# A planned four-layer graph network: planner constants and order tables made anew

## The chip, the cores and the metric

The kernel runs on one core of a Trainium2 chip, as one launch. The metric is the device time of that launch in microseconds. Three runs of the kernel before gave 2421.40, 2421.62 and 2425.13 us, median 2421.62.

## What is computed

128 graphs of 128 nodes with 512 features go through four graph layers; after each the input is added back and the rows are layer-normalised. x is (128, 128, 512), adj (128, 128, 128), everything in float32. Cut to what matters:

```python
x = layernorm(x + relu(An @ x @ K + b))          # layer 0, An = D^-1/2 (adj + I) D^-1/2
x = layernorm(x + softmax_n(w) * (x @ Wv.T))     # layer 1, w = sum_m (q k^T / 8 * adj)
x = layernorm(x + relu(cat(x, adj @ x / deg) @ W.T))   # layer 2
x = layernorm(x + An @ (x @ W3 + b3))            # layer 3
```

The outputs are the last x, (128, 128, 512).

## The kernel before

**Tiling.** Four graphs form a group; there are 32 groups, numbered 0 to 31. One group's x is a tile of 128 partitions (nodes) by four graphs of 512 features. The weight products use a scheme of seven block products in place of eight: each weight is kept as seven blocks of 128 x 2 x 256 (`B11`, `T1`, ..., line 31), the sums of blocks of the data (names with `s1`, `s2`, `s4`, `xT1s`, `xT2s`, `agg0s`, `agg3s`, `inners`) are made by VectorE and GpSimd, and seven products, numbered 0 to 6, are accumulated for each tile. So `p_o0:3` is the fourth unit of matmuls of the layer 0 product of a group, `p_v` that of layer 1, `p_2x` and `p_2g` those of layer 2, `p_o3` that of layer 3, and `p_agg0`, `p_agg3` are the products with the adjacency.

**Weights.** Layer 0's and layer 3's weights, with their sums, do not stay on chip: they are stored once to a scratch tensor in DRAM (`w0d`, `w3d`; function `keep`, line 1009) and fetched again in seven pieces of 256 KB for each group into `wz_sb` (`fetch`, line 1013). A third scratch tensor, `w2d`, holds part of layer 2's weight. Layer 2's weight comes in pieces of 32 KB into `wa_sb`, `wb_sb`, `wc_sb` and `w2y` (`load_w2`, line 1024); `w2_sums` (line 1035) adds the blocks.

**Loops.** After a start with the first groups, a loop over t (lines 1760 on) records layers 0 and 1 of group t beside layers 2 and 3 of group t−1, so in the steady part four layers of work of two groups stand side by side: one such period is one group's time.

**Transposes** of x for layers 1 and 2 mostly go by DMA through a scratch tensor in DRAM (store `xT1s`/`xT2s`, load `xT1y`/`xT2y`, then a block transpose on VectorE into `xT`; `turn_x`, line 1169); in the first groups and the last they are done on PE (`p_xT1`, `p_xT2`; `turn_on_tensor`, line 1183). The adjacency with its scale is `ana`, transposed `anT`; `arT` is the plain one transposed; `sa` and `ya` carry it through a scratch tensor for the attention scores. `p_w`, `scr`, `e_sb`, `p_ws` are the softmax of layer 1; `square`, `last1o`, `last3o`, `last4o`, `mvo`, `rstdo` belong to the layer norms.

**What sets the order.** Nothing is issued as the program text is read. Every call is recorded as an operation of a plan (`Plan.record`, line 666). `Plan.schedule` (line 704) then builds due times, moves some operations to another engine, and `Plan.run` (line 783) plays all operations against a cost estimate and writes down the order in which each engine would take them. `Plan.emit` (line 887) issues them in that order; each engine then works through its own list strictly in order, and an operation that waits holds up all that stand behind it. Since all are issued from `emit`, nearly every row of the profile has line 890, and names of tiles tell the operations apart. Five things steer the plan:

- `estimate` (line 914) gives each operation its duration; for a DMA an issue time on SyncE, 400 ns here, and a size from the length of its runs (`PACKET`).
- `HEAD, BUS` (line 641): in the plan a DMA's data moves at the rate `BUS[0]` if it is issued in the first 40000 ns, at `BUS[1]` after that. `FLIGHT` limits the DMAs under way, `LAND` is added to each.
- `EARLY` (line 33) has a number for each operation of a group, in units of 100 ns, by which its due time is put forward or back. Keys are engine, name and count, such as `s:sa:0c`. A last letter tells the group: `w` for operations of no group (weights), `a`, `b`, `c` for groups 0, 1, 2, none for 3 to 29, `y` for 30, `z` for 31. The first letter is the engine the operation was recorded for (`g` GpSimd, `v` VectorE, `s` ScalarE or SyncE, `t` PE).
- `MOVED` (line 419) lists operations that `move` (line 766) hands to another engine: a sum between VectorE and GpSimd, a copy or a normalisation from ScalarE to VectorE.
- `TIMES` (line 457) fixes, for groups 3 to 29, the order of each engine: an offset for each operation, repeated every `PERIOD` of 73637 ns for the next group.

Group suffixes are used below where an operation of one of the first groups is meant: `p_2g` of group 0, `p_agg3_0` of group 0 and so on.

Of the kernel before, what the change touches and what calls it, by code (L numbers as in the profile page):

```python
# [33 lines left out]
    "g:agg0:0": 52, "g:agg0:0b": 110, "g:agg0:0c": -35, "g:agg0:0y": -5, "g:agg0:0z": -425, "g:agg0s1:0": 31,  # L34
    "g:agg0s1:0b": 134, "g:agg0s1:0c": 107, "g:agg0s1:0y": 132, "g:agg0s1:0z": 84, "g:agg0s2:0": 12,
    "g:agg0s2:0b": -210, "g:agg0s2:0c": 123, "g:agg0s2:0y": -361, "g:agg0s2:0z": -261, "g:agg0s4:0": -71,
    "g:agg0s4:0b": -79, "g:agg0s4:0c": 87, "g:agg0s4:0y": 360, "g:agg0s4:0z": 859, "g:agg30:0z": 623,
    "g:agg30s1:0z": 410, "g:agg30s2:0z": 646, "g:agg30s4:0z": 77, "g:agg31:0z": -329, "g:agg31s1:0z": 410,
    "g:agg31s2:0z": 392, "g:agg31s4:0z": 766, "g:agg3:0": 131, "g:agg3:0a": 333, "g:agg3:0b": -88, "g:agg3:0c": -110,
    "g:agg3:0y": -322, "g:agg3s1:0": 75, "g:agg3s1:0a": 528, "g:agg3s1:0b": -174, "g:agg3s1:0c": -73,  # L40
    "g:agg3s1:0y": -982, "g:agg3s2:0": 6, "g:agg3s2:0a": 24, "g:agg3s2:0b": 233, "g:agg3s2:0c": -16,
    "g:agg3s2:0y": 633, "g:agg3s4:0": 130, "g:agg3s4:0a": -4, "g:agg3s4:0b": 225, "g:agg3s4:0c": -489,
    "g:agg3s4:0y": -118, "g:arT:0": -6, "g:arT:0a": 45, "g:arT:0b": -500, "g:arT:0c": -40, "g:arT:0y": -264,
    "g:arT:0z": -170, "g:arT:1": 52, "g:arT:1a": -19, "g:arT:1b": -120, "g:arT:1c": -597, "g:arT:1y": -412,
    "g:arT:1z": 241, "g:d:0": 24, "g:d:0a": 202, "g:d:0b": 597, "g:d:0c": -98, "g:d:0y": 479, "g:d:0z": 577,
    "g:inner:0": 28, "g:inner:0a": -23, "g:inner:0b": 33, "g:inner:0c": -161, "g:inner:0y": -103, "g:inner:0z": -9,
    "g:inner:1": 32, "g:inner:1a": 163, "g:inner:1b": 49, "g:inner:1c": -147, "g:inner:1y": -81, "g:inner:1z": 158,
    "g:inner:2": 62, "g:inner:2a": 14, "g:inner:2b": 333, "g:inner:2c": 228, "g:inner:2y": -362, "g:inner:2z": -769,
    "g:inners1:0": -21, "g:inners1:0a": 207, "g:inners1:0b": 311, "g:inners1:0c": -84, "g:inners1:0y": 211,
    "g:inners1:0z": 1020, "g:inners1:1": 69, "g:inners1:1a": -28, "g:inners1:1b": -19, "g:inners1:1c": 429,  # L50
    "g:inners1:1y": -160, "g:inners1:1z": 52, "g:inners2:0": 6, "g:inners2:0a": 42, "g:inners2:0b": 316,
    "g:inners2:0c": -125, "g:inners2:0y": 934, "g:inners2:0z": 495, "g:inners2:1": 27, "g:inners2:1a": 22,
    "g:inners2:1b": 597, "g:inners2:1c": -319, "g:inners2:1y": 431, "g:inners2:1z": 201, "g:inners4:0": 15,
    "g:inners4:0a": 206, "g:inners4:0b": -185, "g:inners4:0c": 151, "g:inners4:0y": -376, "g:inners4:0z": -365,
    "g:inners4:1": 4, "g:inners4:1a": 46, "g:inners4:1b": 343, "g:inners4:1c": 17, "g:inners4:1y": 855,
    "g:inners4:1z": 35, "g:last3o2_0:0": -2, "g:last3o2_0:0a": -168, "g:last3o2_0:0b": -312, "g:last3o2_0:0c": 71,
    "g:last3o2_0:0y": -1126, "g:last3o2_0:0z": -8300, "g:last3o2_0:1": -5, "g:last3o2_0:1a": -191,
    "g:last3o2_0:1b": 131, "g:last3o2_0:1c": -27, "g:last3o2_0:1y": -274, "g:last3o2_0:1z": -11, "g:last3o2_0:2": -4,
    "g:last3o2_0:2a": -32, "g:last3o2_0:2b": 253, "g:last3o2_0:2c": 125, "g:last3o2_0:2y": 103,
    "g:last3o2_0:2z": -362, "g:last3o3_0:0": 15, "g:last3o3_0:0a": -230, "g:last3o3_0:0b": -70,  # L60
    "g:last3o3_0:0c": -256, "g:last3o3_0:0y": -437, "g:last3o3_0:0z": -808, "g:last3o3_0:1": 22,
    "g:last3o3_0:1a": 380, "g:last3o3_0:1b": -258, "g:last3o3_0:1c": -80, "g:last3o3_0:1y": 1086,
    "g:last3o3_0:1z": 703, "g:last3o3_0:2z": -4121, "g:last3o3_0:3z": 2795, "g:last3o3_1:0z": -1845,
    "g:last3o3_1:1z": 1419, "g:last4o2_0:0": 6, "g:last4o2_0:0a": -46, "g:last4o2_0:0b": -18, "g:last4o2_0:0c": 320,
    "g:last4o2_0:0y": 1210, "g:last4o2_0:0z": 8290, "g:mean_w3:0w": 2, "g:mean_wv:0w": 265, "g:rs:0": -117,
    "g:rs:0a": -100, "g:rs:0b": -43, "g:rs:0c": 86, "g:rs:0y": -127, "g:rs:0z": 357, "g:rstdo0_0:0": 25,
    "g:rstdo0_0:0a": -173, "g:rstdo0_0:0b": 183, "g:rstdo0_0:0c": -144, "g:rstdo0_0:0y": -134, "g:rstdo0_0:0z": -584,
    "g:rstdo0_0:1": 10, "g:rstdo0_0:1a": 160, "g:rstdo0_0:1b": 126, "g:rstdo0_0:1c": 291, "g:rstdo0_0:1y": 1688,
    "g:rstdo0_0:1z": 572, "g:rstdo0_1:0": 36, "g:rstdo0_1:0a": -417, "g:rstdo0_1:0b": 180, "g:rstdo0_1:0c": 120,
    "g:rstdo0_1:0y": -1819, "g:rstdo0_1:0z": -632, "g:rstdo0_1:1": 28, "g:rstdo0_1:1a": 463, "g:rstdo0_1:1b": 20,  # L70
    "g:rstdo0_1:1c": -257, "g:rstdo0_1:1y": 3996, "g:rstdo0_1:1z": 1836, "g:rstdo3_1:0z": -238, "g:rstdo3_1:1z": 2729,
    "g:v1_0:0": 175, "g:v1_0:0a": -3, "g:v1_0:0b": -122, "g:v1_0:0c": 161, "g:v1_0:0y": 536, "g:v1_0:0z": 159,
    "g:v1_0:1": 53, "g:v1_0:1a": -235, "g:v1_0:1b": -130, "g:v1_0:1c": -458, "g:v1_0:1y": -20, "g:v1_0:1z": -54,
    "g:v1_1:0": 2, "g:v1_1:0a": -127, "g:v1_1:0b": -359, "g:v1_1:0c": 283, "g:v1_1:0y": 352, "g:v1_1:0z": 545,
    "g:v1_1:1": -20, "g:v1_1:1a": 3, "g:v1_1:1b": -110, "g:v1_1:1c": 140, "g:v1_1:1y": 268, "g:v1_1:1z": 73,
    "g:v2_0:0": -25, "g:v2_0:0a": -357, "g:v2_0:0b": -330, "g:v2_0:0c": 69, "g:v2_0:0y": -202, "g:v2_0:0z": 138,
    "g:v2_1:0": -30, "g:v2_1:0a": 50, "g:v2_1:0b": 165, "g:v2_1:0c": -151, "g:v2_1:0y": 1510, "g:v2_1:0z": 553,
    "g:w2y1:0w": -79, "g:wa_sb:0w": -55, "g:wb_sb:0w": 48, "g:wb_sb:1w": -280, "g:wb_sb:2w": -90, "g:wb_sb:3w": -170,
    "g:wc_sb:0w": 73, "g:wc_sb:1w": 11, "g:wc_sb:2w": 88, "g:wc_sb:3w": -88, "g:wc_sb:4w": -224, "g:wc_sb:5w": -90,
    "g:xT1:0": -66, "g:xT1:0a": 56, "g:xT1:0b": 74, "g:xT1:0c": -108, "g:xT1:0y": -179, "g:xT1:0z": 469,  # L80
    "g:xT1s1:0": 17, "g:xT1s1:0a": 259, "g:xT1s1:0b": 113, "g:xT1s1:0c": 400, "g:xT1s1:0y": 2729, "g:xT1s1:0z": 1624,
    "g:xT1s2:0": -8, "g:xT1s2:0a": 40, "g:xT1s2:0b": -109, "g:xT1s2:0c": -136, "g:xT1s2:0y": -182, "g:xT1s2:0z": 378,
    "g:xT1s4:0": 19, "g:xT1s4:0a": 169, "g:xT1s4:0b": 19, "g:xT1s4:0c": 3, "g:xT1s4:0y": 257, "g:xT1s4:0z": 172,
    "g:xT2:0": 25, "g:xT2:0a": -1190, "g:xT2:0b": 137, "g:xT2:0c": 150, "g:xT2:0y": -641, "g:xT2:0z": -64,
    "g:xT2:1": 16, "g:xT2:1a": -52, "g:xT2:1b": 897, "g:xT2:1c": 58, "g:xT2:1y": 446, "g:xT2:1z": 651, "g:xT2:2": -34,
    "g:xT2:2a": 54, "g:xT2:2b": -83, "g:xT2:2c": -165, "g:xT2:2y": -342, "g:xT2:2z": 141, "g:xT2s1:0": -35,
    "g:xT2s1:0a": 70, "g:xT2s1:0b": 46, "g:xT2s1:0c": 37, "g:xT2s1:0y": 387, "g:xT2s1:0z": 406, "g:xT2s1:1": 33,
    "g:xT2s1:1a": 218, "g:xT2s1:1b": -344, "g:xT2s1:1c": -47, "g:xT2s1:1y": -1221, "g:xT2s1:1z": -832,
    "g:xT2s2:0": -40, "g:xT2s2:0a": -588, "g:xT2s2:0b": 149, "g:xT2s2:0c": 18, "g:xT2s2:0y": -308, "g:xT2s2:0z": -283,
    "g:xT2s2:1": 47, "g:xT2s2:1a": -167, "g:xT2s2:1b": -30, "g:xT2s2:1c": 52, "g:xT2s2:1y": 1667, "g:xT2s2:1z": 876,  # L90
    "g:xT2s4:0": -25, "g:xT2s4:0a": 166, "g:xT2s4:0b": 536, "g:xT2s4:0c": 103, "g:xT2s4:0y": -764, "g:xT2s4:0z": -38,
    "g:xT2s4:1": 7, "g:xT2s4:1a": -394, "g:xT2s4:1b": -490, "g:xT2s4:1c": 106, "g:xT2s4:1y": -226, "g:xT2s4:1z": 354,
    "s:agg0:0": -59, "s:agg0:0a": -100, "s:agg0:0b": -22, "s:agg0:0c": 4, "s:agg0:0y": 53, "s:agg0:0z": -429,
    "s:agg0:1": 5, "s:agg0:1a": 213, "s:agg0:1b": -168, "s:agg0:1c": -216, "s:agg0:1y": 347, "s:agg0:1z": -324,
# [535 lines left out]
class Plan:  # L630
# [7 lines left out]
    HOP = {"tensor": 150, "vector": 40, "scalar": 40, "gpsimd": 95, "sync": 35}  # L638
    CLOSE = 500
    LAND, FLIGHT = 1700, 9  # L640
    HEAD, BUS = 40000, (0.65, 1)
    PACKET = {32: 16, 128: 33, 256: 82, 512: 102}

    def __init__(self, tc, est):
# [1180 lines left out]
```

## Time and profile before

| quantity | value |
|---|---|
| median of three runs | 2421.62 us |
| profiled execution, its own time | 2425.63 us |
| its span (first to last instruction) | 2423.8 us |
| busy: PE, PE weight load, VectorE | 2358.1, 1938.4, 1759.7 us |
| busy: ScalarE, GpSimd | 1103.7, 1269.4 us |
| granted clock of PE, mean over the span | 0.995 |
| DMA, share of 16 engines, mean rate | 60.7%, 172 GB/s |
| matmuls, DMAs issued on SyncE | 11244, 1809 |

The profiled execution took 4.0 us more than the median of the runs. Its span leaves 1.8 us around it. PE is PE's matmuls, PEld its weight loads, which overlap them; DVE is VectorE, ACT ScalarE, POOL GpSimd, SP SyncE, whose queue issues all the DMAs. Matmul ends are modelled, so PE's busy time is not the time at its peak; the distances between matmul starts are taken instead where a peak rate is wanted. In a row of the timeline, the figure in brackets is how long the engine stood idle before the operation, and what released it.

### The profile page before, as it was taken

Reading aid. Unit: us, or ns where it says so; the run is one execution under the profiler, and the core shown is the slowest. Engines: PE = TensorE matmul, PEld = TensorE weight load, DVE = VectorE, ACT = ScalarE, POOL = GpSimd, SP = SyncE. Lnnn points to the kernel's source line nnn. Section 1 sums busy time; section 2 is a strip of 40 time slices with the busy share of each in tenths; the row PEclk is TensorE's granted clock in tenths of the full one; section 3 lists DMA queues with packets and bytes.
Section 4 is the critical chain, followed back from the end, with each engine's and each line's share of the span. In section 5 each row is a group of like instructions: output and inputs, shape, how many; then the busy total and the mean of one; then the engine's idle time right before and its main releaser. Section 6 shows DMA issues by size and latency. Waiting matters only on the chain. (4 is left out here: it accounts for less than half of the span.)

```text
span 2423.8 us, 35397 instructions
## 1 busy us (share of the span) xinstructions
PE 2358.1 (97%) x11244; PEld 1938.4 (80%) x11244; DVE 1759.7 (73%) x3611; ACT 1103.7 (46%) x2480; POOL 1269.4 (52%) x1571
## 2 busy tenths in 40 slices
PE   8989999999999999999999999999999999999997
PEld 6767778888878878788878888888888888888776
DVE  5876777677777767777776777777776777777776
ACT  4444444444444445444444444444444444444444
POOL 4345465445565455565455555455654455654434
PEclk9999999999999999999999999999999999999998
DMA  5455575666666665666666756665756675756532
GB/s 148 160 154 162 139 210 167 182 171 183 174 200 166 181 182 170 190 187 172 178 180 174 196 166 182 173 195 168 200 169 180 171 190 169 202 163 189 155 113 79
DMA packets 492106, 417.36 MB, mean 172 GB/s; under 512 B 151824, under 2 KB 375312, under 8 KB 491664
## 3 DMA queue, kind: packets, MB, share of 16 engines
q1 hardware_dynamic: 491920, 415.09, 60.7%
q8 instruction: 91, 1.49, 0.3%
q14 instruction: 95, 0.78, 0.1%
HBM read 297.27 MB, written 117.70 MB: 171 GB/s over the span
## 5 line engine op out<-in xcount | busy, mean ns | idle before, releaser
L890 PE MATMUL p_o<-wz_sb,agg 128*128 128x256 f32 x2048 | 477.5, 380 | 10.0 <-DMA wz_sb<-w0d 3.9
L890 PEld LDWEIGHTS p_o<-wz_sb,agg 128*128 128x128 f32 x2048 | 383.7, 190 | 70.3 <-DMA wz_sb<-w0d 10.9
L890 PE MATMUL p_v<-wv_sb,xT 128*128 128x320 f32 x1024 | 297.1, 433 | 1.3 <-DVE xT L890 1.1
L890 PEld LDWEIGHTS p_agg<-anT,x 128*128 128x128 f32 x2048 | 251.7, 196 | 22.9 <-DVE x L890 8.8
L890 PE MATMUL p_agg<-anT,x 128*128 128x128 f32 x2048 | 257.7, 281 | 9.6 <-DVE x L890 7.0
L890 PEld LDWEIGHTS p_v<-wv_sb,xT 128*128 128x128 f32 x1024 | 191.6, 190 | 87.5 <-DVE xT L890 8.7
L890 ACT COPY agg<-p_agg 128x512 f32<-128x512 f32 (+1 forms) x221 | 116.2, 527 | 252.4 <-PE p_agg L890 251.8
L890 PE MATMUL p_v<-wv_sb,xT1s 128*128 128x320 f32 x768 | 228.1, 433 | 1.5 <-POOL xT1s L890 1.1
L890 PEld LDWEIGHTS p_v<-wv_sb,xT1s 128*128 128x128 f32 x768 | 145.2, 190 | 69.9 <-issue 15.1
L890 PE MATMUL p_o<-wz_sb,agg0s 128*128 128x256 f32 x768 | 183.9, 383 | 11.1 <-DMA wz_sb<-w0d 7.6
L890 DVE TENSOR_TENSOR y<-p_2x,y 128x512 f32<-128x512 f32 (+1 forms) x256 | 158.9, 621 | 38.7 <-PE p_2x L890 34.2
L890 POOL TENSOR_TENSOR y<-u,y 128x1024 f32<-128x1024 f32 (+1 forms) x89 | 178.9, 2010 | 15.0 <-DVE u L890 6.0
L890 PE MATMUL p_o<-wz_sb,agg3s 128*128 128x256 f32 x744 | 176.1, 380 | 1.3 <-POOL agg3s L890 1.3
L890 ACT COPY f_2x<-p_2x 128x512 f32<-128x512 f32 (+1 forms) x122 | 64.7, 531 | 246.4 <-PE p_2x L890 239.8
L890 PEld LDWEIGHTS p_o<-wz_sb,agg0s 128*128 128x128 f32 x768 | 142.6, 190 | 42.8 <-issue 16.9
L890 ACT COPY p_2x<-p_2x 128x512 f32<-128x512 f32 (+1 forms) x216 | 109.1, 516 | 115.5 <-PE p_2x L890 67.6
L890 PEld LDWEIGHTS p_o<-wz_sb,agg3s 128*128 128x128 f32 x744 | 138.9, 190 | 20.2 <-POOL agg3s L890 2.5
L890 POOL TENSOR_TENSOR agg3s<-agg 128x512 f32<-128x512 f32 x29 | 36.7, 1267 | 204.6 <-ACT agg L890 202.2
L890 DVE TENSOR_TENSOR v<-p_v,f_v 128x320 f32<-128x320 f32 x128 | 57.5, 485 | 115.0 <-PE p_v L890 114.8
L890 POOL TENSOR_TENSOR agg<-agg 128x512 f32<-128x512 f32 (+1 forms) x32 | 39.7, 1240 | 190.1 <-DVE x L890 158.6
L890 PE MATMUL p_2g<-y,arT 128*128 128x512 f32 x256 | 121.6, 595 | 2.9 <-DVE y L890 1.8
L890 ACT COPY p_o<-p_o 128x512 f32<-128x512 f32 (+1 forms) x96 | 54.1, 564 | 148.2 <-PE p_o L890 144.4
(233 smaller groups left out, 5322.7 us busy)
## 6 DMA issues: line engine op xcount, KB each, us to landing
wz_sb<-w2d SPq DMA_DIRECT2D x224, 256.0 KB, 3.5
wz_sb<-w3d SPq DMA_DIRECT2D x224, 256.0 KB, 3.8
wz_sb<-w0d SPq DMA_DIRECT2D x203, 256.0 KB, 4.1
x<-in_x_dram SPq DMA_DIRECT2D x31, 1024.0 KB, 5.8
out_dram<-x SPq DMA_DIRECT2D x31, 1024.0 KB, 5.1
xT1s<-x SPq DMA_DIRECT2D x120, 256.0 KB, 2.8
xT1y<-xT1s SPq DMA_DIRECT2D x240, 128.0 KB, 2.7
xT2s<-x SPq DMA_DIRECT2D x120, 256.0 KB, 2.7
```

Of the source, the lines that this page charges most:

```text
L890: op.ins = getattr(getattr(self.nc, op.engine), method)(*[v.real() if isinstance(v, Ref) else v for v in args], **{k: v.real() if isinstan ...
```

## The change

Three things differ. The plan's assumed DMA rate for the first 40 us goes from 0.65 to 1.1. A DMA with runs of 256 elements and a size over 1000 in the planner's measure is given 600 ns to issue, no longer 400. And the tables `EARLY`, `MOVED` and `TIMES` hold new numbers throughout: not only the keys of the weights and of groups 0, 1 and 2, but also those of the middle groups and of groups 30 and 31. `PERIOD` stays 73637. The program that records the operations is the same; the number of operations, all the matmuls and all the DMAs are unchanged. Only their order on each engine differs, and for some the engine.

```diff
@@ tables @@
 EARLY = {
-    "g:agg0:0": 52, "g:agg0:0b": 110, "g:agg0:0c": -35, "g:agg0:0y": -5, "g:agg0:0z": -425, "g:agg0s1:0": 31,
...
 TIMES = {
...
     "te": {
-        "p_agg0_3:0": -15388, "p_agg0_1:0": -14793, "p_agg0_0:0": -14186, "p_agg0_2:0": -13424, "p_o0:1": 3745,
-        "p_o0:0": 4975, "p_o0:2": 5558, "p_o0:3": 7384, "p_o0:4": 9773, "p_o0:5": 10599, "p_o0:6": 14335,
...
+        "p_agg0_3:0": -15888, "p_agg0_1:0": -15493, "p_agg0_0:0": -14586, "p_agg0_2:0": -13824, "p_o0:1": 5345,
+        "p_o0:0": 5875, "p_o0:2": 6558, "p_o0:3": 7284, "p_o0:4": 7973, "p_o0:5": 8899, "p_o0:6": 10935,
...
@@ Plan @@
-    HEAD, BUS = 40000, (0.65, 1)
+    HEAD, BUS = 40000, (1.1, 1)
...
@@ estimate @@
     if method == "dma_start":
...
-        return 400, Plan.LAND + size, size, False
+        return 600 if run == 256 and size > 1000 else 400, Plan.LAND + size, size, False
```

As the planned orders come out of it (in each, what stood before and what stands now):

- GpSimd, start: d, ana+ident, ana·d, b0; now ana+ident, d, ana·d, b0. The first ana+ident was tied behind VectorE's dm and is now tied behind dh.
- SyncE, start: ana, b0, wz, x (graphs 2, 3), wz, x (graphs 0, 1) sixth; now ana, x (graphs 0, 1), b0, x (graphs 2, 3), then the four wz pieces.
- SyncE, later: the store `sa` of group 2 stood ahead of most of layer 2's weight pieces, now behind them; the stores of w0d and w3d and the pieces of `wc_sb` come earlier among the others.
- PE, middle groups: 16 of some 72 units stand at another place. Among them, p_o3:3 now stands ahead of p_o0:0, and p_o3:6 ahead of p_o0:3, directly behind p_2x0:0.
- VectorE, middle groups: x of graph 2, row 0 (`x:5`) ahead of `x:7`; `x:19` behind xT2:1, where it stood between xT2:0 and xT2:1.
- Engines, each middle group: three copies of p_o0, f_v_0 and v0 go from VectorE to ScalarE, one normalisation (`x:2`) from ScalarE to VectorE; the sums agg0s4:0, xT1s2:0, arT:0, xT2:1 go from VectorE to GpSimd, inner:0 and xT2:2 from GpSimd to VectorE.

## The prediction

> **What bounds the kernel now.** I read the page first (busy shares), then the table of stretches, then PE's waits, then the timeline where the waits are long. The page and the stretches (columns: stretch, length, then busy us and instructions of PE, weight load, VectorE, ScalarE, GpSimd, then granted clock, DMA share, GB/s):
>
> ```profile
> PE 2358.1 (97%) x11244; PEld 1938.4 (80%) x11244; DVE 1759.7 (73%) x3611; ACT 1103.7 (46%) x2480; POOL 1269.4 (52%) x1571
> ...
> 0.00:20.00 20.00, 13.43 (x76) 12.24 (x76) 5.36 (x12) 4.41 (x9) 7.94 (x15) 0.91 0.84 246
> 20.00:40.00 20.00, 17.20 (x98) 15.17 (x99) 13.80 (x30) 4.93 (x11) 7.93 (x10) 1.00 0.58 171
> ...
> 80.00:100.00 20.00, 20.00 (x105) 16.04 (x103) 16.74 (x28) 8.72 (x20) 7.31 (x7) 1.00 0.31 95
> 100.00:120.00 20.00, 15.87 (x68) 12.38 (x68) 17.14 (x32) 2.24 (x5) 13.45 (x14) 1.00 0.50 162
> 120.00:140.00 20.00, 18.20 (x78) 13.60 (x76) 16.06 (x28) 6.73 (x11) 9.40 (x16) 1.00 0.38 115
> 140.00:160.00 20.00, 11.74 (x54) 10.08 (x53) 12.72 (x38) 11.42 (x29) 4.57 (x8) 0.74 0.81 193
> ```
>
> TensorE bounds it. A 128x256 matmul starts 216 ns after the one before when PE is fed, 128x320 269, 128x512 429, 128x128 111 (starts in the trace); over all matmuls that is 2318.2 of the 2423.8 us span. The matmuls are the same 11244 afterwards, so only the other 105.6 us can move. They lie so: 48.0 before 320 us, about 30 from 320 to 2200, 19.7 after that, and 7 behind the last matmul. PE's waits to 240 us, and from 320 to 2200 us (total, times, longest):
>
> ```profile
> PE p_w L890 <- DVE scr L890: 6.1, 1, 6.1
> PE p_a L890 <- POOL ana L890: 3.4, 1, 3.4
> PE p_o L890 <- DVE u_o L890: 3.4, 3, 1.7
> ...
> PE p_o L890 <- DMA wz_sb<-w0d: 8.7, 27, 1.0
> PE p_2x L890 <- DVE xT L890: 3.7, 8, 1.0
> ```
>
> The head waits for single late things; a middle group (73.6 us) loses only 1.1 to 1.2 us. **The change part by part.** Nothing computed is added or removed: two planner constants change and the tables are new, so order and engine of operations move, in all 32 groups. I walk the new orders with the old durations.
>
> *First 18 us.* GpSimd's old order (timeline: start, length):
>
> ```profile
> 4.67 1.03 POOL L890 TENSOR_TENSOR d<-dh,nhalf 128x4 f32<-128x4 f32 x1 [3.38 <-DVE dh L890]
> ...
> 7.64 1.26 POOL L890 TENSOR_TENSOR ana<-ana,ident 128x512 f32<-128x512 f32 x1 [1.93 <-issue]
> 8.97 1.04 POOL L890 TENSOR_TENSOR ana<-ana,d 128x512 f32<-128x512 f32 x1
> ...
> 10.07 0.66 PE L890 MATMUL p_a<-ident,ana 128*128 128x128 f32 x4 [3.37 <-POOL ana L890]
> ...
> 11.59 5.45 PE L890 MATMUL p_agg<-anT,x 128*128 128x128 f32 x32 [0.86 <-DVE anT L890]
> ```
>
> GpSimd sat still 1.93 us because ana+ident stood behind VectorE's dm (7.50), not for its data. Now ana+ident goes first, behind dh (4.59): 4.67 to 5.93, d to 7.01, ana·d to 8.08, p_a at 8.13 instead of 10.07: **−1.9**. x of graphs 0 and 1 is SP's second issue instead of its sixth; its 512 KB take 5.7 us, so it is there. The wz pieces go back two to four places of 0.6 us and land by about 12.
>
> *Clock.* PE ran at 0.5 from 11.59 to 15.0 here, so the first two graphs' p_agg took 1.87 and 1.63 us, the others 0.89: 1.7 lost. [...] I take half, **−0.9** (ends 0 and −1.9).
>
> *18 to 60.* The four p_agg come earlier and p_o follows in an order whose VectorE copies are ready: by the walk p_agg of group 1 starts near 28.9 (34.7 before), and at 53 us PE is 6 ahead, since 5.4 us of p_v are done earlier in the old gaps (20 to 40 us lost 2.7). SP stood still over 17 us for a store:
>
> ```profile
> 36.21 0.88 SPq L890 DMA_DIRECT2D wa_sb<-in_L_gnn_W_dram  x2
> 54.70 1.31 SPq L890 DMA_DIRECT2D sa<-ana  x2
> ```
>
> The 50-odd 32 KB pieces of layer 2's weights were behind that store; now most go ahead of it at 0.46 us each, and w0d's store near 41 (70.36 before). Price: GpSimd's first wb sum waits for a piece near 55.5, with group 1's rstdo behind it on GpSimd, and PE's transposes of group 1 (p_xT1, 66.5 before) behind that row: **+1.4**. Lead at 60: about 5.
>
> *60 to 140.* w3d's store goes near 63 (77.34), so the sixteen wc pieces that follow land near 80 instead of 93.6. The old sums came in a lump behind them, which is why VectorE is 17.1 of 20 busy exactly where PE is only 15.9:
>
> ```profile
> 93.74 1.23 DVE L890 TENSOR_TENSOR wc_sb<-w2y,wc_sb 128x1024 f32<-128x1024 f32 x1 [0.60 <-DMA wc_sb<-in_L_gnn_W_dram]
> 95.10 2.35 POOL L890 TENSOR_TENSOR wc_sb<-wc_sb,wb_sb 128x1024 f32<-128x1024 f32 x1 [2.68 <-DVE wc_sb L890]
> ...
> 108.43 1.99 PE L890 MATMUL p_o<-wz_sb,agg 128*128 128x256 f32 x8 [1.69 <-DVE u_o L890]
> ```
>
> Spread over 80 to 110 they leave most of the 1.7 + 1.4 + 0.8 us that PE waited for u_o and p_2x between 100 and 120: −3; three new waits for GpSimd's and VectorE's single weight sums, 1.0 + 0.9 + 0.4, give +2.3 back near 112; the wait for w2d's fetch (117 to 122 before) comes earlier with its store: −1.5. Lead at 126: about 9 with all the clock gain, 8 with half.
>
> *140 to 156.* p_w waited 6.1 us, at half clock after it, for scr, which shares a buffer with the squares. The same chain (p_2g, x, four squares, last3o, x) is there in the new order and only starts earlier; ScalarE normalises graph 0's x ahead of graph 1's, which p_agg wants first: −0.7. From 156 to 320 the old order lost about 10 more; I can't walk it to 1 us: 0, ends −3 and +3. **Head: −8.7**, less 1 for the small waits a walk doesn't see: −7.7.
>
> *Middle groups, 27 times.* Each engine swap is one for one within 0.1 us of total: three VectorE copies of 0.48 to 0.68 go to ScalarE (46% busy) and one of 0.80 comes back; three adds go to GpSimd at 1.2 against 0.7 and two come back at 0.7 to 1.3. VectorE, 73% busy, and GpSimd, 52%, hide them; uncovered, one costs its 0.7 us a group. The wait for w0d's fetch at the second p_o tile stays. The one at p_o0:3 (7.1 us in all) goes, as three tiles now stand ahead of it. x of graph 2, row 0, moves ahead on VectorE, so the transposing DMA behind it lands about 0.7 earlier and p_2x0:0's wait (6.6 in all) mostly goes. Against that p_o3:6 now stands right behind p_2x0:0 and needs x:19, which VectorE does behind two xT2 sums, no longer one. Each takes 0.62 from start to start, p_2x0:0 covers 0.4 of it: up to 0.85 us a group; after the 0.55 that the earlier landing spares it is 0.3, 8 in all, or 0.5 and 13 if the DMA lands little earlier. So −5.7, or +6 with that worse end; not seen in the trace, I take a third of the good: **−2**. Tail: −3 to +3, 0 taken.
>
> **Sum**: −7.7 − 2 = −9.7 on the profiled 2425.6, which lies 4.0 above the median of 2421.6: 2415.9 there, **2412** for the median.
>
> **Rivals.** (a) *The lead is lost again* behind the weight sums or the chain at 140, since nothing there is shorter: for it, that chain of 9 us is pure latency; against it, it starts when p_2g ends, earlier. Leaves the 0.7 and 1: 2420. (b) *Only the first 18 us pay*, 1.9 + 0.9, with w2d's fetch as late as before: 2418.5. (c) *Slower: x:19 on VectorE.* If the DMA lands no earlier and PE has no slack there, it waits the whole 0.85 us a group, 23 in all; less the 7.7 of the head and the 7.1 of p_o0:3: +8, 2430. It decides from 0.55 us a group on (14.8 in 27). For it, VectorE is the second busiest and p_o3:6 has no matmul of another tile before it; against it, the sums are due just ahead of the DMA's landing. (d) The constants alone change no program; that nothing moves is out, as the order does.
>
> **Numbers.** Likeliest (head's lead kept, middle within ±6) 0.61, own range 2404 to 2417; (b) 0.11, (a) 0.15, (c) 0.13. 0.2%, 4.8 us, is about what tells from no change. Faster takes the likeliest and half of (b): 0.67; same the rest of (b), (a) and a little of (c): 0.21; slower 0.12. The range leaves out the far side of (c) and gains over 20: 2402 to 2424.
>
> **What would show it.** p_a near 8.1 with GpSimd's 1.93 gone; full clock from 9.6; no SP gap at 37 to 54; w3d near 63; PE over 17 busy in 100 to 120; p_w's 6 us still there, near 132. In the middle, p_o0:3 without w0d and p_o3:6 with a wait for x under 0.4. Wrong if p_2g of group 1 isn't 7 to 10 earlier, or if a middle period is over 73.9.

## The result, and the profile after

The changed kernel takes 2395.14 us (median of four runs, 2393.32 to 2397.90) against 2422.74 for the kernel before on the same chip: a ratio of 0.9886, 95% interval 0.9869 to 0.9903, 27.6 us less. Timed again beside another kernel it had 0.9898 (0.9884 to 0.9912). The forecast was 2412, 9.7 us less, with a range of 2402 to 2424: the sign was right, the size about a third of what came.

The page of the changed kernel:

```profile
PE 2351.7 (98%) x11244; PEld 1941.6 (81%) x11244; DVE 1704.6 (71%) x3506; ACT 1129.1 (47%) x2536; POOL 1306.3 (55%) x1620
```

The matmuls are as many as before; what went is the time between them. To see where, I compare the two traces at equal work: the matmuls done by a given time in the old trace (each counted at its full-rate distance), and how much earlier the new trace has done as many. That is PE's lead, in us:

| old trace's time | 26 | 35 | 60 | 105 | 115 | 126 | 155 | 320 | 1000 | 2200 | 2410 |
|---|---|---|---|---|---|---|---|---|---|---|---|
| lead | 6.3 | 1.6 | 3.2 | 2.2 | 5.2 | 4.5 | 7.1 | 10.1 | 18.0 | 26.7 | 27.1 |

The head gave 10.1, the groups from 320 to 2200 us gave 16.6, the tail 0.4. For the same work, the time between matmuls over full-rate distance fell there from 29.9 to 13.4 us. These are single traces; other kernels with the old tables in the middle lose 28.3 (e11), 27.9 (e10) and 23.9 us (e2) from 320 to 2200, five traces more with the new ones 14.6 to 16.2 (the changed kernel 14.9), so the gain is no chance of two traces, but its size is known to some us only. PE's waits there, after:

```profile
PE p_o L886 <- DMA wz_sb<-w0d: 1.0, 5, 0.3
PE p_o L886 <- DVE x L886: 0.4, 1, 0.4
```

Before, these were 8.7 us for w0d and 3.7 for xT at p_2x. (The list leaves out the shortest waits. In the distances between matmul starts, p_o0:1 went from 9.4 to 6.2 over 25 groups, p_2x0:0 from 5.4 to 0, p_o0:3 from 5.5 to 0, p_o0:2 from 1.8 to 0, and up to 0.1 us a group more went on the matmul behind each.) In the head, the table of stretches after, columns as in the prediction:

```profile
20.00:40.00 20.00, 15.94 (x85) 13.30 (x84) 13.27 (x29) 11.30 (x33) 7.45 (x10) 0.91 0.59 180
...
100.00:120.00 20.00, 18.36 (x80) 14.37 (x79) 17.83 (x33) 3.45 (x7) 12.34 (x19) 1.00 0.60 197
120.00:140.00 20.00, 14.17 (x58) 9.72 (x56) 14.79 (x39) 9.55 (x19) 10.57 (x15) 0.95 0.47 134
```

100 to 120 is the better stretch that was forecast (15.87 before); 20 to 40 is worse than before (17.20). The waits to 240 us:

```profile
PE p_w L886 <- DVE scr L886: 5.2, 1, 5.2
PE p_o L886 <- DVE u_o L886: 3.3, 2, 2.8
```

and the timeline of the places that the steps of the prediction spoke of:

```profile
4.75 1.27 POOL L886 TENSOR_TENSOR ana<-ana,ident 128x512 f32<-128x512 f32 x1 [3.46 <-DVE dh L886]
...
8.20 0.65 PE L886 MATMUL p_a<-ident,ana 128*128 128x128 f32 x4 [1.53 <-POOL ana L886]
...
10.28 3.84 PE L886 MATMUL p_agg<-anT,x 128*128 128x128 f32 x32 [1.43 <-DVE anT L886]
...
24.95 0.36 DVE L886 COPY wv_sb<-wqk_sb 128x128 f32<-128x128 f32 x2 [2.42 <-DMA wqk_sb<-in_L_gnn_W_qk_dram]
...
28.11 3.29 PE L886 MATMUL p_o<-wz_sb,agg 128*128 128x256 f32 x8 [2.84 <-DVE u_o L886]
...
57.28 3.13 SPq L886 DMA_DIRECT2D sa<-ana  x4
```

GpSimd's idle 1.93 us are gone and p_a starts at 8.20. At 24.95 VectorE has waited 2.42 us for a weight's DMA, with u_o behind that copy and p_o0:6 behind u_o: 2.84 us of PE. From 28.58 to 32.00 the granted clock is 0.5, so p_o0:6 itself takes 3.29 us (the eight equal matmuls at 23.37, at full clock, 1.89). The old 17 us hole in SyncE's queue is gone; w0d's store goes at 42.4, w3d's at 65.9.

For the middle groups, SyncE's queue and PE in one period. Before:

```profile
1401.07 0.38 SPq L890 DMA_DIRECT2D xT2s<-x  x1
1401.81 0.33 SPq L890 DMA_DIRECT2D wz_sb<-w0d  x1
1402.99 0.92 SPq L890 DMA_DIRECT2D xT2s<-x  x2
...
1415.34 0.70 PE L890 MATMUL p_2x<-wb_sb,xT 128*128 128x256 f32 x2 [0.53 <-DVE xT L890]
```

After:

```profile
1380.94 1.63 SPq L886 DMA_DIRECT2D xT2s<-x  x2
1382.68 0.45 SPq L886 DMA_DIRECT2D wz_sb<-w0d  x1
1383.22 1.98 SPq L886 DMA_DIRECT2D xT2s<-x  x2
...
1393.90 0.59 PE L886 MATMUL p_2x<-wb_sb,xT 128*128 128x256 f32 x2
```

Both stores of x's row 0 now go ahead of w0d's block for p_o0:0, and later ones likewise. Over 25 groups, measured from p_o3:5's start (medians): the fourth and last piece of xT2y of row 0, which p_2x0:0 needs, is issued at −3.6 instead of −2.4 us and lands at 0.9 instead of 2.4, while w0d's block for p_o0:0 lands at −4.4 instead of −5.8. p_o0:0 itself starts at −3.5, no longer at −5.2, because p_o3:3 stands ahead of it.

### The profile page after: what moved, and what is told of

It is laid out like the page before. It is cut to its first block, busy times and chain, and to the rows that moved or that the text cites. A ratio compares the mean times of both kernels' runs of the same rounds, so it can differ in the third digit from the quotient of the medians.

```text
span 2396.1 us, 35384 instructions
## 1 busy us (share of the span) xinstructions
PE 2351.7 (98%) x11244; PEld 1941.6 (81%) x11244; DVE 1704.6 (71%) x3506; ACT 1129.1 (47%) x2536; POOL 1306.3 (55%) x1620
## 5 line engine op out<-in xcount | busy, mean ns | idle before, releaser
L886 PE MATMUL p_v<-wv_sb,xT 128*128 128x320 f32 x1024 | 302.3, 433 | 0.2 <-DVE v L886 0.2
```

Of the source, the lines that this page charges most:

```text
L886: op.ins = getattr(getattr(self.nc, op.engine), method)(*[v.real() if isinstance(v, Ref) else v for v in args], **{k: v.real() if isinstan ...
```

## Experiments

Parts of the tables were put back or put in alone. Lead and waits below come from each kernel's profiled execution, ratios from all its runs against the kernel before on the same chip. Ratios of 0.001 are 2.4 us.

### Middle alone, head alone

e1 is the kernel before with the new tables for groups 3 to 29, e2 the kernel before with the new constants and the new keys of the weights and groups 0 to 2.

```diff
 e1:  EARLY, MOVED: keys without a last letter, and all of TIMES   <- new; the rest old
 e2:  EARLY, MOVED: keys ending in w, a, b, c; HEAD/BUS, estimate  <- new; the rest old
```

> The kernel before with the new tables for groups 3 to 29 only (all of TIMES, and the keys of EARLY and MOVED without a last letter); constants, weights, groups 0 to 2, 30 and 31 as before. Theory 1, the middle groups' order is worth 16 to 17 us: 2406, between 2403 and 2409, and the waits for w0d and for xT at p_2x together under 2 us in 320 to 2200. Theory 2, the middle is worth what the prediction gave it, 2 to 6, and the rest of the gain comes down from the head's lead: 2417 to 2421.

> The two constants and the new keys of EARLY and MOVED with the letters w, a, b, c; the middle groups, 30 and 31 as before. Theory 1: the head gives its 10 us and nothing else, 2412, between 2410 and 2415, with the waits of the middle (w0d 9 us, xT at p_2x 4 us) back. Theory 2: the lead of the head also takes the waits of the middle away, 2397 to 2402.

e1 took 2432.84, ratio 1.0049 (1.0033 to 1.0065); e2 2426.95, 1.0026 (1.0015 to 1.0036). Neither theory had foreseen that both would be slower than before. The lead tells why. In e1, PE lost 15.7 us between matmuls from 330 to 2190, as against 29.9: the new middle is worth its 14 us without the new head. But between 240 and 280 us, where the hand-over from groups planned by EARLY to groups planned by TIMES lies, it fell 13.6 us behind, 16.7 by 360, and 8.5 more between 2200 and 2300, at the other hand-over. PE's waits of e1 from 225 to 330 us:

```profile
PE p_v L893 <- POOL xT1s L893: 9.9, 2, 5.5
```

In e2 the lead was 6.6 at 220 us (7.3 in the changed kernel), then 12.1 behind at 280, with 8.1 us of the same wait. So a half of the tables can't be joined to the other half: the seam costs more than the half brings. The sum of the two experiments says nothing of the change; their stretches away from the seams do.

### The queue, and the order of the matmuls

e3 is the changed kernel with SyncE's old order in groups 3 to 29; e4 has the old order of PE there; e5 and e6 put back one place of each.

```diff
 e3:  TIMES["sy"]  <- old            e4:  TIMES["te"]  <- old
 e5:  TIMES["te"]["p_o3:3"]:  behind p_o0:0
 e6:  TIMES["sy"]["w0d:0"]:   between xT2s_0:0 and xT2s_0:1
```

> The changed kernel with the old order of SyncE's queue in groups 3 to 29 (the sy part of TIMES), every other engine's order as changed but for 3 operations on VectorE and 2 on ScalarE near group 30. Theory 1, it is the queue that brings the transposing DMAs and w0d earlier: xT2y's last piece lands about 0.8 later against p_o3:5, p_2x0:0 or p_o3:6 waits 0.3 to 0.5 us a group again, and the time is 2403 to 2410. Theory 2, the new order of the matmuls and of x:5 on VectorE does it: under 2 us more, 2395 to 2397.

> The changed kernel with the old order of the matmuls in groups 3 to 29 (the te part of TIMES), SyncE's queue as changed; 14 operations of VectorE, 6 of ScalarE and 2 of SyncE move with it. Theory 1: with w0d and xT2y landing earlier the old order waits little, 1 to 3 us more, 2396 to 2398. Theory 2: p_o0:3 waits for w0d again, 7 us, and with p_2x0:0 up to 13: 2402 to 2408.

> The changed kernel with one pair of PE units in groups 3 to 29 put back: p_o0:0 stands ahead of p_o3:3 again. SyncE's queue is as changed. Theory 1: the pair is what lets the queue send w0d's block for p_o0:0 later; without it p_o0:0 waits 0.7 to 1.0 us a group and the time is 2412 to 2420. Theory 2: the 20 us of p_o0:0 seen with the old matmul order came from other units that moved as well: under 4 us more, 2396 to 2399.

> The changed kernel with one DMA of groups 3 to 29 put back in SyncE's queue: w0d's block for p_o0:0 goes ahead of the second store of xT2s of row 0 again. All else as changed. Theory 1: this place is most of what the queue brings; xT2y lands 0.4 to 0.7 us later and p_2x0:0 and p_o3:6 wait again for a part of the 23 us that the old queue cost: 8 to 16 us more, 2403 to 2411. Theory 2: the later places (w0d:2 behind both stores of row 1, the order of the xT2y loads) make it: under 4 us more.

e3: 2418.36, ratio 0.9992 (0.9981 to 1.0003): the whole gain is gone but for 2 us, though up to 2052 us every engine but SyncE has the changed kernel's order. PE's waits of e3 from 320 to 2200 us:

```profile
PE p_o L888 <- DVE x L888: 6.8, 15, 0.5
PE p_2x L888 <- DVE xT L888: 6.0, 12, 1.0
PE p_o L888 <- DMA wz_sb<-w0d: 2.8, 7, 0.8
```

In start-to-start distances that is 9.9 + 2.1 us at p_o3:6 (waiting for x:19), 8.3 + 1.5 at p_2x0:0 and 3.6 at p_o0:2, as in the kernel before or more; the last piece of xT2y of row 0 lands at 2.7 (2.4 before), although x:5 keeps its new place on VectorE. Theory 1 holds, at about twice its price.

e4: 2431.38, ratio 1.0042 (1.0028 to 1.0057), 36 to 38 us above the changed kernel, where theory 1 had 1 to 3 and theory 2 up to 13. Its waits there:

```profile
PE p_o L888 <- DMA wz_sb<-w0d: 17.6, 27, 1.2
PE p_2g L888 <- POOL y L888: 6.1, 25, 0.4
```

It is p_o0:0 that waits, 20.3 us of start-to-start time, for the block that the new queue sends about a place later; p_2g_2 costs 10.2 more. Both theories had it too small. e5 shows that one pair is enough for most of it: 2417.97, ratio 0.9985 (0.9975 to 0.9995), 24 us of the 38, with p_o0:0 at 18.2 + 2.5 us and p_o0:1 at 8.4 (6.2 in the changed kernel). Theory 1 holds. p_o3:3 ahead of p_o0:0 is the 1.73 us that lets the queue put the transposes first.

e6: 2405.04 (two runs), ratio 0.9931 (0.9911 to 0.9951), about 11 us of the 25 that e3 lost; in its one trace the lead at the end is 7 less than the changed kernel's. Only SyncE's order differs. p_o3:6 waits 5.4 + 1.0 us:

```profile
PE p_o L888 <- DVE x L888: 3.7, 10, 0.5
```

Theory 1 holds, and the groups of one trace show the link one by one. In 10 of e6's 25 groups the last xT2y of row 0 lands 2.1 to 2.7 us after p_o3:5's start, and in these p_o3:6 waits 0.4 to 0.74 us; in the other 15 it lands by 0.82, and PE doesn't wait. In e3 it lands later than 1.8 in 18 groups, with waits of 0.3 to 0.74; in the changed kernel in one, with 0.65.

### Two places alone, and a third exchange

e11 puts just those two places into the kernel before. e8 was to exchange one more pair in the changed kernel, to cover the wait that is left at p_o0:1. But its tables also hold the edit of e5 (p_o3:3 behind p_o0:0), so e5 is what it has to be compared with.

```diff
 e11 (on before):  TIMES["sy"]["w0d:0"]: behind xT2s_0:1;  TIMES["te"]["p_o0:0"]: behind p_o3:3
 e8 (on changed):  TIMES["te"]["p_o0:1"]: 5345 -> 5400, behind p_o3:2
                   TIMES["te"]["p_o3:3"]: 152772 -> 153162, behind p_o0:0   # as in e5
```

> The kernel before with two places changed in groups 3 to 29: w0d's block for p_o0:0 behind the second store of xT2s of row 0 in SyncE's queue, and p_o3:3 ahead of p_o0:0 on PE to cover it. Theory 1: these two together are the core of the middle's gain; the transposes land 0.4 to 0.6 us earlier, the wait at p_2x0:0 (6.6 us) goes and p_o0:0 does not wait: 5 to 9 us less, 2412 to 2417. Theory 2: without the rest of the queue and of the matmul order they bring nothing or move the wait to p_o0:2 and p_o0:3: 2419 or more.

> The changed kernel with one pair of PE units in groups 3 to 29 exchanged: p_o3:2 ahead of p_o0:1, so that a unit of 1.73 us covers w0d's first block, for which p_o0:1 still waits 0.25 us a group and streams 0.07 slower. Theory 1: that wait goes, 6 to 8 us in all: 2387 to 2390. Theory 2: the product p_o0:1 is copied out later and VectorE and ScalarE hold up what comes behind, or p_o3:2 waits for its own sums: 2394 or more.

e11: 2423.67, ratio 1.0022 (1.0013 to 1.0032): nothing gained, 5 us lost. The last xT2y of row 0 lands at 2.5, as before, while the later stores and loads of xT2 are still mixed with w0d's other blocks, and p_o0:0 (3.2), p_o0:3 (5.8) and p_o0:1 (10.5) wait. Theory 2. Taking one of the places out costs about 11 or 24 us, putting both in alone brings nothing: these two need the rest of the new order.

e8: 2420.57, ratio 0.9997 (0.9988 to 1.0006), 27 us above the changed kernel, but e5's edit alone is 24 above it; against e5 it is 3 us, and the intervals overlap. Its waits from 320 to 2200:

```profile
PE p_o L888 <- ACT p_o L888: 17.9, 25, 0.7
PE p_o L888 <- DMA wz_sb<-w0d: 7.3, 10, 1.0
```

p_o3:2 waits for ScalarE's copy of p_o, 0.88 us in every group: with p_o0:1 moved away, nothing stands between it and p_o3:0 to hide that copy. That is a wait of the kind theory 2 named. Since it delays p_o0:0 too, it covers half of e5's wait there (10.5 us of 20.7 are left). What the exchange alone would do to the changed kernel, no run shows.

### The head

e10 is the kernel before with nothing but the two constants. e7 takes the two wqk copies on VectorE and puts them behind u_o. e9 adds SyncE and GpSimd: sa of group 2 earlier, the first wb sum behind group 1's rstdo. For both, the finished plan is edited and not planned anew:

```diff
+LATER = (copies "s:wv_sb:0w", "s:wv_sb:3w" on VectorE  -> behind "v:u_o0:1a"        # e7, e9
+         11 weight pieces on SyncE -> behind "s:sa:3c"; 4 more -> behind "s:ya:2c"   # e9
+         "g:wb_sb:0w" on GpSimd -> behind "g:rstdo0_1:1b")                           # e9
 def emit(self):
-    for op in self.schedule():
+    done = self.schedule()
+    for late, then in LATER:
+        done = self.later(done, late, then)
+    for op in done:
```

> The kernel before with the two constants (rate 1.1, 600 ns for the larger pieces) and all its own tables. Theory 1: the constants do nothing by themselves but upset an order that the old tables were made for; the head is 0 to 6 us worse, 2421 to 2428, the middle unchanged. Theory 2: the better rate alone makes a better head: 2412 to 2417.

> The changed kernel with two copies on VectorE (wqk into wv_sb, which waited 2.4 us for their DMA at 22.5 to 24.9 us) put behind both u_o of group 0; nothing else moves. Theory 1: the head's lead of 6.3 us at 26 fell to 1.6 at 35 because of this wait and the half clock after it; p_o0:6 of group 0 then starts 1.8 to 2.2 earlier, at full clock, and 2 to 4 us of it reach the end: 2391 to 2393. Theory 2: what comes next (the transposes of group 0, weights) is not ready any earlier and takes it back: within 1 us of the changed kernel.

> The changed kernel with the copies of e7 behind u_o, the four sa stores of group 2 moved up by eleven 32 KB pieces in SyncE's queue (to right behind ana of group 2), four more pieces behind the ya loads, and GpSimd's first wb sum put behind group 1's rstdo. Theory 1, the head is gated by what SyncE brings and by that sum: ya lands near 64 instead of 67, PE is 2 to 3 us further ahead at 70 than in e7, and 2 to 3 us reach the end: 2392 to 2393. Theory 2: the next wait (weight sums near 105 to 116, or the chain at 132 to 142) takes it back: 2394 to 2396.

e10: 2437.26, ratio 1.0078 (1.0048 to 1.0108), 18 us slower, outside both expectations but on theory 1's side: by 200 us it is 20 behind, in a row of new waits of 1 to 3 us, and the middle is as before. The constants give nothing without tables made for them; what they bring within the new set is open, as no run has the new tables with the old constants.

e7: 2394.96, ratio 0.9886 (0.9870 to 0.9903), no different from the changed kernel. p_o0:6 waits 1.3 us, not 2.8, at full clock, and the lead at 35 is 4.1, not 1.6. The copies are only a part of that: e3 and e4, with the same head and no half clock there, lose 3.4 and 3.2 between 26 and 35, the changed kernel 4.7, e7 1.6. So the copies cost 1.6 to 1.8 of it, and the stretch of half clock at 28.58 about 1.4. At 65 e7's lead is 2.5, as in the changed kernel (2.1): PE's transposes of group 1 wait 2.0 us for a row whose rstdo stands on GpSimd behind a wb sum, which waits until 58.7 us. Theory 2.

e9: 2394.29, ratio 0.9904 (0.9889 to 0.9918). ya lands earlier and the lead at 65 is 5.2, at 320 13.0; but these ratios don't tell it from the changed kernel. So both were timed together:

> The changed kernel itself, unedited, on the same chip as the next one. Both theories: 0.9886 of the kernel before, 2391 to 2396 if that stands at 2419 to 2423.

> The kernel of e9 once more beside the changed kernel. Theory 1, the 2.9 us of lead that its trace showed over the changed one at 320 us reach the end: 2 to 4 us under e12. Theory 2: the spread of the DMAs from run to run (2 to 4 us) swallows them or the middle takes them back: within 1 us of e12.

e12 (the changed kernel) 2396.88, e13 (e9 again) 2395.80, ratios 0.9898 (0.9884 to 0.9912) and 0.9895 (0.9881 to 0.9909). In this pair of traces the leads were 2.8 and 4.3 at 65 us, 11.1 and 11.7 at 320, 28.0 and 29.8 at the end. About 1 us: the places moved do what was said of them, but no measured gain over the changed kernel can be claimed. It is near theory 2, but that the 2 to 4 us between runs come from the DMAs was not shown; e12's six runs lie 3.9 us apart (2395.01 to 2398.88).

## Why the prediction was wrong

**First 18 us: right.** p_a started at 8.20 (8.13 predicted, 10.07 before). p_agg started at 10.28, not at 9.6, as VectorE copied the bias into p_o twice first (1.29 us from 8.27, its anT at 9.54).

**Clock: the half I counted was an estimate, and the gain doesn't last.** This trace has the full clock from 10.28 to 28.58. e12 is the same program, and at half clock it took 1.87 and 1.55 us for the first two graphs' p_agg (start to start) before 0.89. With e5, e6 and e8 that is four executions at half and seven at full clock among eleven whose order is the same up to 25 us (granted clock from 12 to 16 us: 0.62, 0.64, 0.72 and 0.79 in e5, e6, e8 and e12, 1.00 in the changed kernel's first trace). With one order the stretch of half clock came in some executions and not in others, and what decides it was not shown. So no run shows the 0.9 that the sum takes. What they showed in its place: at 26 us the four at half clock lead by 4.4 to 4.8 and the seven others by 5.7 to 6.7, but at 320 us nothing of that can be told: e12, e5, e6 and e8 lead by 11.1, 11.5, 10.0 and 10.4, the changed kernel by 10.1.

**18 to 60: wrong in size.** Predicted 6 at 53 and 5 at 60; measured 2.8 and 3.2. The walk had no DMA of wqk in front of u_o, and p_agg of group 1 starts at 32.97, not near 28.9 (34.67 before). The wb sum was right: the lead falls from 3.2 to 2.1 between 60 and 65, 1.1 for a price of 1.4.

**60 to 140: right where it gains, short at the end.** The weight sums no longer come in a lump, and the lead grows by 3.0 between 105 and 115, as said. At 126 it is 4.5, not 8 to 9; of the 3.5 missing against 8, 1.8 were missing at 60 already.

**140 to 156, and to 320: low.** The chain is there, and PE waits from 134 on (near 132 forecast), 5.2 + 2.2 us at p_w and p_ws (6.1 + 1.3 before); from 135 to 155 the lead grows by 1.9 (0.7 predicted), and from 155 to 320 by 3.0, for which the sum took 0. The head in all: 10.1, predicted 7.7.

**Middle groups: the step that failed.** The prediction took 2 us; it is 16.6, and this is 14.6 of the 17 us between forecast and result. Taking a third of the good end accounts for 3.7 of them; the rest was in the terms. The term for p_o3:6 and x:19 ("after the 0.55 that the earlier landing spares it is 0.3, 8 in all") measured 0.6 us. With it p_2x0:0's wait vanished, not "mostly", p_o0:2's went as well, and the one at p_o0:1 that "stays" fell by 3.2. Added up with what was right (p_o0:3, 7.1): 7.1 + 6.6 + 2.2 + 3.2, less 3.1 of start-to-start time new at the first p_2g and 0.6 at p_o3:6, is 15.4 of the 16.6; the rest are waits under 1 us. The wrong term came from the landing of xT2y: I moved it by the 0.7 us that x:5 moves on VectorE. It moved 1.5, because SyncE's queue sends the transposes ahead of w0d's blocks in each group, and I had followed that queue only through the head. With the old queue, e3, it lands no earlier at all, x:5 or not, and my term is real: p_o3:6 costs 12 us, at most 0.74 in a group for the 0.85 counted, and p_2x0:0 nearly 10. My worse end, "0.5 and 13 if the DMA lands little earlier", is what e3 measures at p_o3:6, on a kernel that does not have the new queue. I also counted three sums that go to GpSimd; four go, and none shows as a wait.

**Its signs.** p_a, SyncE's gap, w3d (65.9), 100 to 120 us, p_o0:3 and p_o3:6 came out as named, and a middle period is 72.6 us on the mean (73.3 before). p_2g of group 1 starts only 5.4 us earlier and ends 9.4 earlier, where 7 to 10 were asked. Signs that are met did not tell a middle worth 2 us from one worth 16.6.

**Rivals.** (b), only the first 18 us pay, is out: the lead is 3.9 at 18 us and 10.1 at 320. (c), slower through x:19, was the right mechanism for e3's kernel and did not come about here. (a), the lead lost in the head, came about in part between 26 and 35. (d), that the constants alone change no program, is wrong as put: e10 shows that they alone move the head's order, for the worse.

What stays open: why the planner's new head gains 3 us from 155 to 320, which no run took apart, how the 25 us that e3 loses divide among the queue's places beyond the one that e6 puts back (about 11 of them), and what the two constants are worth with the new tables.

## What to carry to other kernels

Where several engines run lists made together, follow every list through the repeating part before pricing a wait in it, the DMA queue first: in e6 p_o3:6 waited 0.4 to 0.74 us in the 10 groups where the last xT2y landed 2.1 to 2.7 us after p_o3:5's start, and not in the 15 where it landed by 0.82. That one place in the queue was worth about 11 us, one pair of matmuls 24, over 27 groups. Such orders are worth what they are worth as a set: half of a new order joined to half of an old one was slower than either (e1 2432.84, e2 2426.95 us), and the seam showed as large waits in the trace (9.9 us at p_v in e1, 8.1 in e2). A gain in the start-up phase can end at a later wait: e7 led by 4.1 us at 35, where the changed kernel led by 1.6, and at 65 by 2.5 to 2.1. To see whether one survives, compare the work done at a later time, not the time of one instruction.

## What the runs showed of the hardware

The same program began with TensorE at full clock in one profiled execution and at half clock from about 10.2 to 13.7 us in another (e12). In e12 the 3.44 us before that held 1.57 us of matmuls, busy and idle in turns (columns as in the prediction):

```profile
6.80:10.24 3.44, 1.57 (x12) 1.09 (x10) 2.49 (x5) 0.49 (x3) 1.63 (x3) 1.00 1.04 369
10.24:13.65 3.41, 3.24 (x15) 3.24 (x16) 0.11 (x1) 1.69 (x3) 0.79 (x2) 0.50 0.89 201
```

It cost 1.6 us at 16 us. At 35 us e12 led by 0.7 more than the first trace, which had its own half clock from 28.58 to 32.00, and at 320 by 1.0 more.

The changed kernel's first trace has the granted clock 0.50 from 28.58 to 32.00 and from 137.81 to 148.05 us as well. Why the clock halves where it does, no run shows.

Two traces of the kernel of e9 differ by 1.3 us in lead at 320, with equal instructions in equal order: executions of one program differ by about as much as the last experiments tried to win.
